# A four-layer graph network on one core: the last block of nodes on 32-row tiles, fewer packing stages in narrow chunks, narrower fetches

## The chip, the cores and the metric

The kernel runs on one core of a Trainium2 chip. The metric is the device time of one execution in microseconds (us), lower is better. Three executions of the kernel before took 2365.87, 2366.54 and 2370.38 us, so the median is 2366.54 us. A profile is one further execution, with its own time. In it, PE is TensorE's matmul, PEld its weight load, DVE is VectorE, ACT is ScalarE, POOL is GpSimd and SP is SyncE, which issues most of the transfers.

## What is computed

There are N = 2708 nodes with 512 features each, and an adjacency matrix adj of zeros and ones, in which a row has about sixteen ones. Four layers follow each other; each adds its result to its input and normalises each row. Cut to what matters:

```python
deg = max((adj != 0).sum(-1), 1)
x = layernorm(x + relu(((adj + I) @ x / deg + x) @ W0 + b0))        # layer 0
x = layernorm(x + (dis[:, None] * adj * dis[None, :]) @ x @ W1.T + b1)  # layer 1
for W in W_stack:                        # layer 2: two attention layers on x
    Wh, Ws = split(y @ W)
    a = softmax(Wh @ Ws.T) * adj
    y = leaky_relu(a @ Wh + y)
x = layernorm(x + y)
x = layernorm(x + adj @ x @ W3 + b3)                                # layer 3
```

Layer 0 scales both sides of adj by the square root of the degree, which is not written out here; dis is the inverse square root of adj's row sum.

## The kernel before

**Blocks and chunks.** The 2708 nodes are padded to 22 blocks of 128. The last block, number 21, holds only 20 real nodes; the other 108 rows of it are zeros. The columns of adj are cut into six chunks (CH, L28): four of 512 columns, one of 384 and one of 276. The blocks form six groups (GROUPS, L30): four groups of four blocks, then two of three, so block 21 is the last of the last group.

**Layers 0, 1 and 3.** For each chunk k and each group g, in this order, step() (L1001) is called. It first readies the next group (before_products, which calls load, L724, for the group after the next, and prepare, L757, for the next), then issues the products of this group (multiply, L821), then one part of the end of the chunk before (ends, L1036: multiplication by the weights, layernorm, storing). A run.phase counts these parts: it is 0 after the first group of a chunk, and so on.

**The products with adj.** The rows x of a block are split into a high and a low half in a reduced format (halve, L713: ACT makes xh, DVE makes xl), so that two fast matmuls give the accuracy of a slow one. For a chunk there are four accumulators acc in PSUM, one for each quarter d of the 512 features, each a bank of its own. For each block there are four times two matmuls with 128 rows of contraction, xh or xl as stationary operand and m, the block's piece of adj, as moving operand.

**Where m comes from.** Layer 0 loads adj transposed (at<-in_adj_t on SP), casts it to m on ACT, checks it on DVE (odd), adds up degrees (part) and writes it as bytes to a scratch in DRAM (masks; POOL casts and stores). Layers 1 and 3 and the attention read those bytes again (at<-mask, a<-mask). In layer 1, prepare also reduces the bytes on DVE to feeds: for each node, whether it feeds any node of each quarter (32 columns) of each block.

**The packing job.** index() (L1054) turns feeds of a chunk into lists of the nodes that feed a block of 128 nodes. Each block has eight lists of 128 places for nodes that feed one quarter only (two for each quarter) and four for the rest. The job is a generator in stages: a DVE stage, then a PE stage, in turn. First rank, then rest (both count places with matmuls), then for each block of the chunk one list: DVE builds a one-hot matrix (at_row, hit, both), PE sums it up (22 matmuls into list), and DVE copies the sum out of PSUM (sums), behind the one-hot of the list after it. The jobs of layer 1's chunks form a queue. work("PE") and work("DVE") advance the first job by one stage if it is that engine's turn. In layer 1, step() calls them at four places each in a chunk. What is left runs in the attention part, where beat() is called after each piece of work and advances a DVE stage and a PE stage every third time. A list must be there before the chunk is used in the attention.

**The attention.** Scores sp are computed by chunks, made into weights s by exp, multiplied by adj, and stored in DRAM next to the features: pairs holds for each pair of blocks and each node one row of 128 weights for the even block, 512 features, and 128 weights for the odd block. fetch() (L1524) gathers 128 such rows of one list by an indirect transfer on POOL into a tile g: the first or the last 640 elements of the row. weigh() (L1568) multiplies: for one of the rest lists one matmul with 128 columns of weights; for the four quarter lists of one turn, four matmuls, each with 32 columns of weights and an own 32 rows of PSUM (128*32 in the profile), next to each other.

**Order.** The Ordered wrapper (L53) fixes each engine's order to the order in which the program is written, so nothing is moved by a scheduler; line 70 stands for nearly every instruction in the profile, and groups are told apart by their tiles.

Of the kernel before, what the change touches and what calls it, by code (L numbers as in the profile page):

```python
# [513 lines left out]
class Fast:  # L514
# [198 lines left out]
    def halve(self, ly, j):  # L713

        nc = self.nc
        hi = self.page(f"xh{ly.number}_{j}", FR)
        lo = self.page(f"xl{ly.number}_{j}", FR)
        s = self.k.dis[:, j : j + 1] if ly.number == 1 else 1.0
        x = ly.rows[j]
        nc.scalar.activation(hi, x, AF.Copy, scale=s)  # L720
        nc.vector.scalar_tensor_tensor(lo, x, s, hi.bitcast(FP), ALU.mult, ALU.subtract)
        ly.hi[j], ly.lo[j], ly.rows[j] = hi, lo, None

    def load(self, ly, k, g):  # L724

        c0, cw = CH[k]
        if (k, g) in ly.loaded:
            return
        ly.loaded.add((k, g))
        js = range(*GROUPS[g])  # L730
        if ly.number == 0:
            tiles = []
            for j in js:
                at = self.wide(f"at{ly.number}_{k}_{j}")
                self.nc.sync.dma_start(at[:, :cw], self.k.adj_t[bass.ts(j, P), c0 : c0 + cw])
                tiles.append(at)
        else:
            at = self.page(f"at{ly.number}_{k}_{g}", U8, (P, DC, BANK))
            self.nc.sync.dma_start(
                at[:, : len(js), :cw], self.k.masks[k][:, js[0] : js[-1] + 1, :]  # L740
            )
            tiles = [at[:, q, :] for q in range(len(js))]
            ly.done["bytes", k, g] = at
        ly.done["at", k, g] = tiles
        if k == 0 and ly.number == 0:
            for j in range(*GROUPS[g]):
                self.load_rows(ly, j)
        if k == 0 and ly.number == 3 and g < 4:
            for j in range(*GROUPS[g]):
                self.load_rows(ly, j)  # L750
        if ly.number == 0 and g == 2:
            xt = [self.page(f"xt{k}_{c}") for c in range(DC)]
            for c in range(DC):
                self.nc.gpsimd.dma_start(xt[c][:, :cw], self.k.x_t[:, c, c0 : c0 + cw])
            ly.done["xt", k] = xt

    def prepare(self, ly, k, g):  # L757


        nc, (c0, cw) = self.nc, CH[k]  # L760
        ats = ly.done.pop(("at", k, g), None)
        if ats is None:
            return
        ms = []
        for j, at in zip(range(*GROUPS[g]), ats):
            if k == 0:
                self.halve(ly, j)
            m = self.page(f"m{ly.number}_{k}_{j}", FR)
            nc.scalar.copy(m[:, :cw], at[:, :cw])
            ms.append(m)  # L770
        ly.done["m", k, g] = ms
        if ly.number == 0:
            self.examine(ly, k, g, ats)
        if ly.number == 1:
            at, (j0, j1) = ly.done.pop(("bytes", k, g)), GROUPS[g]
            feeds = self.k.feeds.rearrange("p i q j -> p j (i q)")
            i0, full = c0 // QW, cw // QW
            for q0, q1, n in ((0, full, QW), (full, -(-cw // QW), cw % QW)):
                if q0 < q1:
                    v = at[:, : j1 - j0, q0 * QW : q0 * QW + (q1 - q0) * n]  # L780
                    nc.vector.tensor_reduce(
                        feeds[:, j0:j1, i0 + q0 : i0 + q1],
                        v.rearrange("p j (q i) -> p j q i", i=n),
                        AX.X,
                        ALU.max,
                    )

    def examine(self, ly, k, g, ats):
        nc, cw = self.nc, CH[k][1]
        b0 = GROUPS[g][0]  # L790
        if g == 0:
            ly.part[k] = self.page(f"part{k}", BF, (P, 2, BANK))
        odd = self.page(f"odd{k}_{g}", BF)
        at_b = self.page(f"bytes{k}_{g}", U8, (P, DC, BANK))
        for q in range(0, len(ats), 2):
            some = self.page(f"some{k}_{g}_{q}", BF, (P, 2, BANK))
            m = min(2, len(ats) - q)
            for h in range(m):
                at = ats[q + h][:, :cw]
                n = k * NB + b0 + q + h  # L800
                nc.scalar.copy(some[:, h, :cw], at)
                nc.vector.scalar_tensor_tensor(
                    odd[:, :cw],
                    at,
                    1.0,
                    at,
                    ALU.is_equal,
                    ALU.not_equal,
                    accum_out=self.k.bad[:, n : n + 1],
                )  # L810
            nc.gpsimd.tensor_copy(at_b[:, q : q + m, :cw], some[:, :m, :cw])
            p = ly.part[k][:, :m, :cw]
            if b0 + q == 0:
                nc.vector.tensor_copy(p, some[:, :m, :cw])
            else:
                nc.vector.tensor_add(p, p, some[:, :m, :cw])
        nc.gpsimd.dma_start(
            self.k.masks[k][:, b0 : b0 + len(ats), :], at_b[:, : len(ats), :cw]
        )

    def multiply(self, ly, k, g, only=None, ds=range(DC)):  # L821
        nc, cw = self.nc, CH[k][1]
        blocks = only or range(*GROUPS[g])
        two = ly.number == 3 and k < TWO
        starts, stops = ((0, 16), (15, NB - 1)) if two else ((0,), (NB - 1,))
        if blocks[0] in starts and 0 in ds:

            half = 0 if two and blocks[0] == 0 else k
            ly.acc[k] = [self.bank(half, f"acc{ly.number}_{k}_{d}") for d in range(DC)]
        ms = ly.done["m", k, g]  # L830
        todo = [(d, j) for d in ds for j in blocks]
        if k == 0 and g + 1 < len(GROUPS):
            todo.sort(key=lambda a: a[1])
        for d, j in todo:
            for x, first in ((ly.hi, True), (ly.lo, False)):
                nc.tensor.matmul(
                    ly.acc[k][d][:, :cw],
                    x[j][:, bass.ts(d, P)],
                    ms[j - GROUPS[g][0]][:, :cw],
                    start=(j in starts and first),  # L840
                    stop=(j in stops and not first),
                )
# [158 lines left out]
    def step(self, run, t):  # L1001
# [6 lines left out]
        if ly.number == 1 and k == len(CH) - 1 and g in (2, 3, 4):  # L1008
            self.attention.begin(g - 2)
        self.multiply(ly, k, g)  # L1010
        if run.before and run.phase in (1, 3, 4, 5):
            self.work("PE")
        if run.before:
            self.ends(run, run.phase)
            run.phase += 1
            if run.phase in (3, 4, 5):
                self.work("DVE")
        if g == (4 if ly.number == 3 and k < TWO else 3):
            self.residual(ly, k)
# [34 lines left out]
    def index(self, k):  # L1054
# [100 lines left out]
        nc.vector.tensor_single_scalar(part, whole, 7, op=ALU.arith_shift_right)  # L1155
        nc.vector.tensor_copy(which, part)
        sums = tile_("sums", [P, n, 2 * LISTS], FP)
        ps = None
        for q in range(n + 1):
            if q < n:  # L1160
                rows, both = self.one_hot(i0 + q, row[:, q, :], which[:, q, :])
            if ps is not None:
                nc.vector.tensor_copy(sums[:, q - 1, :], ps)
            if q == n:
                break
            yield "PE"
            ps = self.bank(self.other, f"list{i0 + q}", (P, 2 * LISTS))
            for j in range(NB):
                nc.tensor.matmul(
                    ps,  # L1170
                    rows[j // 8][:, j % 8, :],
                    both[:, j, :],
                    start=(j == 0),
                    stop=(j == NB - 1),
                )
            yield "DVE"
        t = tile_("list", [P, n, LISTS], FP)
        nc.vector.scalar_tensor_tensor(
# [58 lines left out]
class Attention:  # L1237
# [286 lines left out]
    def fetch(self, ch):  # L1524
# [5 lines left out]
        if q not in ch.x:  # L1530
# [3 lines left out]
            if ch.ly.number == 1:  # L1534
                ch.first[q] = self.page(f"x1{ch.name}_{q}")
                self.nc.sync.dma_start(ch.first[q][:w], self.k.saved[1][i][:w])
        self.nc.gpsimd.indirect_dma_start(
            out=g,
            out_offset=None,
            in_=ch.ly.pairs[ch.k % 2].rearrange("r j d -> (r j) d"),  # L1540
            in_offset=bass.IndirectOffsetOnAxis(ap=self.k.givers[:, i, t : t + 1], axis=0),
            element_offset=(q // 2) * NP * (D + 2 * P) + (q % 2) * P,
        )

        begin = max(self.fetch_free, self.clock + (16 if (q, t) == ch.first_fetch else 0))
# [22 lines left out]
    def weigh(self, wait=False):  # L1568
# [15 lines left out]
        gs = [ch.fetched.pop(0)[0] for _ in ts]  # L1584
        if first:
            ch.acc = self.bank(1, f"acc{ch.name}_{q}")
        c = (q % 2) * D
        for h, g in enumerate(gs):
            lo, m = (0, w) if len(gs) == 1 else (h * QW, QW)
            nc.tensor.matmul(  # L1590
                ch.acc[lo : lo + m],
                g[:, c + lo : c + lo + m],
                g[:, P - (q % 2) * P : P - (q % 2) * P + D],
                start=first,
                stop=last,
            )
# [206 lines left out]
```

## Time and profile before

| what | value |
|---|---|
| median of three executions | 2366.54 us |
| the profiled execution: its time, its span | 2390.8 us, 2388.9 us |
| mean granted TensorE clock | 0.989 |
| ACT busy, share of the span | 655.3 us, 27% |
| POOL busy, share of the span | 761.0 us, 32% |
| products acc<-m,xh and acc<-m,xl, instructions | 1584 and 1584 |
| moved by the transfers | 471.75 MB |

How to read it: the busy times of the engines overlap, so they don't add up to the span. Layer 0 runs from about 20 to 312 us after the span's start, layer 1 to 636, the attention to about 2170 (with the first products of layer 3 among its end), layer 3 to the end. A matmul of the full-precision kind (scores, weights) shows as two records of 429 ns each at 512 columns.

### The profile page before, as it was taken

The page shows a single profiled execution, that of the slowest core. Times are in us where ns is not written, and L with a number is a line of the kernel's source. Part 1 is how long each engine was busy: PE and PEld are TensorE (multiplying, and loading weights), DVE is VectorE, ACT ScalarE, POOL GpSimd, SP SyncE. Part 2 cuts the span into 40 slices and gives each one's busy share as a digit, 9 for nine tenths or more (in the row PEclk, how much of TensorE's full clock was granted, in tenths as well). Part 3 has the DMA queues.
Part 4 walks back from the last instruction along what each step waited for, and adds up shares of the span by engine and source line. Part 5 has one row for each costly group of instructions (what it writes and reads, how often), then busy time and mean ns, then how long its engine had stood idle before and what let it go on. Part 6 is the DMA issues. An engine that isn't in the chain of part 4 may idle for free.

```text
span 2388.9 us, 26130 instructions
## 1 busy us (share of the span) xinstructions
PE 2305.8 (97%) x8518; PEld 1315.5 (55%) x8518; DVE 1476.1 (62%) x2842; ACT 655.3 (27%) x1300; POOL 761.0 (32%) x879
## 2 busy tenths in 40 slices
PE   9999999999999999999999999999999989899997
PEld 6677777777644444443555344444343445566585
DVE  7989986787655328667667511238778777624513
ACT  6434352222100123222223200123232323431221
POOL 6545541111000001535456450001535556451000
PEclk9999999999999999999999999999999999999999
DMA  9754552222345405869789896405869799882311
GB/s 352 254 185 161 182 171 77 74 82 65 130 159 183 150 0 162 283 215 317 244 299 348 272 397 233 147 5 179 283 209 308 264 301 336 277 288 96 118 49 42
DMA packets 312151, 471.75 MB, mean 197 GB/s; under 512 B 59874, under 2 KB 189418, under 8 KB 312004
## 3 DMA queue, kind: packets, MB, share of 16 engines
q1 hardware_dynamic: 251988, 240.80, 30.7%
q0 software_dynamic: 60016, 229.18, 27.4%
q8 instruction: 69, 1.13, 0.2%
q14 instruction: 78, 0.64, 0.1%
HBM read 316.01 MB, written 153.85 MB: 197 GB/s over the span
## 4 chain that ended last, share of the span: by engine, by line
PE 83%; DVE 7%; issue 4%; DMA 3%; POOL 2%; ACT 1%; SPq 0%; another core or an unknown queue 0%; DVEq 0%; POOLq 0%; ACTq 0%
PE sp L70 30%; PE acc L70 30%; PE mm L70 9%; PE z L70 6%; PE wst L70 6%; POOL g L70 1%; DVE at_row L70 1%; DMA g<-pairs,givers 1%; DVE rs_t L70 1%; DMA at<-in_adj_t 1%; DVE feeds L70 0%; DVE st L70 0%; PE tr_x2b L70 0%; PE tr_x2t L70 0%; PE list L70 0%
## 5 line engine op out<-in xcount | busy, mean ns | idle before, releaser
L70 POOL DMA_INDIRECT g<-pairs,givers x510 | 516.3, 1012 | 922.1 <-issue 593.3
L70 PE MATMUL sp<-xs,wst_sb 128*128 128x512 f32 (+3 forms) x2112 | 798.2, 545 | 0.0
L70 PEld LDWEIGHTS sp<-xs,wst_sb 128*128 128x128 f32 (+1 forms) x2112 | 381.1, 186 | 408.6 <-issue 339.7
L70 PE MATMUL acc<-m,xh 128*128 128x512 f32 (+2 forms) x1584 | 586.8, 376 | 15.4 <-DVE dg L70 4.6
L70 PE MATMUL acc<-m,xl 128*128 128x512 f32 (+2 forms) x1584 | 571.1, 366 | 3.7 <-DVE xl L70 3.7
L70 PEld LDWEIGHTS acc<-m,xh 128*128 128x128 f32 x1584 | 299.3, 189 | 76.2 <-issue 16.1
L70 PEld LDWEIGHTS acc<-m,xl 128*128 128x128 f32 x1584 | 299.6, 189 | 52.5 <-issue 6.5
L70 PE MATMUL acc<-g 128*32 128x512 f32 (+1 forms) x1020 | 266.6, 605 | 6.8 <-issue 5.0
L70 DVE TENSOR_TENSOR top<-top,s 128x512 f32<-128x512 f32 (+5 forms) x240 | 149.4, 623 | 188.3 <-ACT s L70 129.9
L70 ACT COPY s<-sp 128x512 f32<-128x512 f32 (+2 forms) x252 | 133.4, 530 | 474.7 <-PE sp L70 312.6
L70 PE MATMUL mm<-w,ht 128*128 128x512 f32 (+1 forms) x528 | 227.3, 603 | 7.5 <-DVE ht L70 7.5
L70 ACT CAST m<-at 128x512 fp32r<-128x512 uint8 (+5 forms) x396 | 199.1, 566 | 79.2 <-DMA at<-mask 58.7
L70 ACT ACTIVATE s<-s 128x512 f32<-128x512 f32 (+3 forms) x264 | 150.5, 580 | 256.3 <-DVE s L70 169.6
L70 DVE TENSOR_TENSOR sum<-sum,s 128x512 f32<-128x512 f32 (+4 forms) x252 | 156.9, 622 | 38.7 <-ACT s L70 20.3
L70 DVE TENSOR_TENSOR s<-s,a 128x512 f32<-128x512 f32 (+3 forms) x264 | 165.8, 628 | 9.1
L70 PEld LDWEIGHTS mm<-w,ht 128*128 128x128 f32 (+1 forms) x528 | 97.3, 189 | 126.6 <-issue 113.1
L70 DVE TENSOR_TENSOR s<-s,shift 128x512 f32<-128x512 f32 (+3 forms) x264 | 162.7, 619 | 4.0 <-issue 4.0
L70 PE MATMUL wst<-xt,mixed 128*128 128x512 f32 (+2 forms) x384 | 157.2, 563 | 3.5 <-issue 3.5
L70 PEld LDWEIGHTS acc<-g 128*32 128x32 f32 (+1 forms) x1020 | 75.7, 134 | 148.2 <-issue 123.9
L70 PE MATMUL z<-w,xt 128*128 128x512 f32 (+1 forms) x352 | 150.8, 595 | 0.0
L70 POOL DMA_DIRECT2D x<-o x44 | 26.0, 596 | 370.2 <-DVE o L70 366.5
L70 DVE COPY z_sb<-z 128x512 f32<-128x512 f32 (+1 forms) x44 | 30.4, 690 | 179.3 <-PE z L70 140.9
(159 smaller groups left out, 1654.6 us busy)
## 6 DMA issues: line engine op xcount, KB each, us to landing
pairs<-s SPq DMA_DIRECT2D x378, 128.0 KB
pairs<-z_sb SPq DMA_DIRECT2D x84, 512.0 KB
at<-in_adj_t SPq DMA_DIRECT2D x88, 256.0 KB
xres<-x POOLq DMA_DIRECT2D x44, 256.0 KB
x<-o POOLq DMA_DIRECT2D x43, 256.0 KB
x<-x SPq DMA_DIRECT2D x37, 256.0 KB
at<-mask SPq DMA_DIRECT2D x32, 256.0 KB
xt<-t SPq DMA_DIRECT2D x32, 256.0 KB
```

The source lines that it names most:

```text
L70: ins = call(*args, **kw)
```

## The change

There are four parts.

1. **Block 21's products.** Its real nodes fit in 32 rows. In layer 0 its piece of adj is loaded four times, into rows 0 to 31, 32 to 63 and so on; the bytes stored for layers 1 and 3 then have the copies too. The new function fold() puts the four feature quarters of block 21 below each other, so that xh and xl of that block are 128 by 128. multiply() starts the last group with eight matmuls of 32 rows of contraction, two for each quarter d, each on its own 32 rows of the array and into its own accumulator; the others of the group follow. Degrees (part) and feeds count 32 rows of block 21 alone; for that the reduction of the last group is cut in two.
2. **Packing stages.** In chunks narrower than 512 columns, step() calls work("PE") at phases 1 and 5 instead of 1, 3, 4 and 5, and work("DVE") at phase 4 instead of 3, 4 and 5 (the one at the end of a chunk stays).
3. **Sums.** ACT copies a list's sum out of PSUM right after its matmuls; the copies on DVE are gone.
4. **Fetches.** A quarter list's fetch leaves out the weights of quarters that it doesn't use: from the list's own quarter on for an even block, up to and with it for an odd block. The tile's columns in weigh() follow.

```diff
@@ halve, fold @@
+        if j == NB - 1:
+            x, s = self.fold(ly, x, s)
+            hi, lo = hi[:, :P], lo[:, :P]
...
+    def fold(self, ly, x, s):
+        nc = self.nc
+        f = self.page(f"fold{ly.number}")[:, :P]
+        for d in range(DC):
+            nc.scalar.copy(f[d * QW : (d + 1) * QW], x[:QW, bass.ts(d, P)])
+        if ly.number == 1:
+            t = self.small.tile([P, 1], FP, tag="dis_f", name="dis_f")
+            for d in range(DC):
+                nc.vector.tensor_copy(t[d * QW : (d + 1) * QW], s[:QW])
+            s = t
+        return f, s
@@ load @@
-                self.nc.sync.dma_start(at[:, :cw], self.k.adj_t[bass.ts(j, P), c0 : c0 + cw])
+                if j < NB - 1:
+                    self.nc.sync.dma_start(
+                        at[:, :cw], self.k.adj_t[bass.ts(j, P), c0 : c0 + cw]
+                    )
+                    continue
+                few = self.k.adj_t[j * P : j * P + QW, c0 : c0 + cw]
+                for d in range(DC):
+                    self.nc.sync.dma_start(at[d * QW : (d + 1) * QW, :cw], few)
@@ prepare @@
+            sets = [(j0, j1, P)] if j1 < NB else [(j0, j1 - 1, P), (j1 - 1, j1, QW)]
...
-                if q0 < q1:
-                    v = at[:, : j1 - j0, q0 * QW : q0 * QW + (q1 - q0) * n]
+                for a, b, rows in sets if q0 < q1 else ():
+                    v = at[:rows, a - j0 : b - j0, q0 * QW : q0 * QW + (q1 - q0) * n]
                     nc.vector.tensor_reduce(
-                        feeds[:, j0:j1, i0 + q0 : i0 + q1],
+                        feeds[:rows, a:b, i0 + q0 : i0 + q1],
@@ examine @@
-            p = ly.part[k][:, :m, :cw]
+            n = QW if b0 + q == NB - 1 else P
+            p, t = ly.part[k][:n, :m, :cw], some[:n, :m, :cw]
@@ multiply @@
-        starts, stops = ((0, 16), (15, NB - 1)) if two else ((0,), (NB - 1,))
+        starts, stops = ((0, 16), (15, NB - 2)) if two else ((0,), (NB - 2,))
...
+        if blocks[-1] == NB - 1:
+            blocks = blocks[:-1]
+            for x in (ly.hi, ly.lo):
+                for d in range(DC):
+                    few = slice(d * QW, (d + 1) * QW)
+                    nc.tensor.matmul(
+                        ly.acc[k][d][:, :cw],
+                        x[NB - 1][few],
+                        ms[-1][few, :cw],
+                        start=False,
+                        stop=False,
+                    )
@@ step @@
-        if run.before and run.phase in (1, 3, 4, 5):
+        wide = CH[k][1] == BANK
+        if run.before and run.phase in ((1, 3, 4, 5) if wide else (1, 5)):
             self.work("PE")
...
-            if run.phase in (3, 4, 5):
+            if run.phase in ((3, 4, 5) if wide else (4,)):
                 self.work("DVE")
@@ index @@
-        ps = None
-        for q in range(n + 1):
-            if q < n:
-                rows, both = self.one_hot(i0 + q, row[:, q, :], which[:, q, :])
-            if ps is not None:
-                nc.vector.tensor_copy(sums[:, q - 1, :], ps)
-            if q == n:
-                break
+        for q in range(n):
+            rows, both = self.one_hot(i0 + q, row[:, q, :], which[:, q, :])
             yield "PE"
...
+            nc.scalar.copy(sums[:, q, :], ps)
             yield "DVE"
@@ fetch @@
+        h = t // ONLY if t < QUARTERS * ONLY else (0, QUARTERS - 1)[q % 2]
+        first, width = (P, D + (h + 1) * QW) if q % 2 else (h * QW, D + P - h * QW)
         self.nc.gpsimd.indirect_dma_start(
-            out=g,
+            out=g[:, :width],
...
-            element_offset=(q // 2) * NP * (D + 2 * P) + (q % 2) * P,
+            element_offset=(q // 2) * NP * (D + 2 * P) + first,
@@ weigh @@
-        c = (q % 2) * D
         for h, g in enumerate(gs):
             lo, m = (0, w) if len(gs) == 1 else (h * QW, QW)
+            e, z = (D + lo, 0) if q % 2 else (0, P - lo)
             nc.tensor.matmul(
                 ch.acc[lo : lo + m],
-                g[:, c + lo : c + lo + m],
-                g[:, P - (q % 2) * P : P - (q % 2) * P + D],
+                g[:, e : e + m],
+                g[:, z : z + D],
```

More of the change, by code (lines that the diff above doesn't have):

```diff
@@ L811, in examine @@
             nc.gpsimd.tensor_copy(at_b[:, q : q + m, :cw], some[:, :m, :cw])
-            p = ly.part[k][:, :m, :cw]
+            n = QW if b0 + q == NB - 1 else P
+            p, t = ly.part[k][:n, :m, :cw], some[:n, :m, :cw]
             if b0 + q == 0:
-                nc.vector.tensor_copy(p, some[:, :m, :cw])
+                nc.vector.tensor_copy(p, t)
             else:
-                nc.vector.tensor_add(p, p, some[:, :m, :cw])
+                nc.vector.tensor_add(p, p, t)
         nc.gpsimd.dma_start(
```

## The prediction

> **What bounds the kernel now.** I read the page's busy table and slices first, then TensorE's groups by shape, the windows by stage, TensorE's waits, and last the timeline where it waits.
>
> ```profile
> PE 2305.8 (97%) x8518; PEld 1315.5 (55%) x8518; DVE 1476.1 (62%) x2842; ACT 655.3 (27%) x1300; POOL 761.0 (32%) x879
> ...
> DVE  7989986787655328667667511238778777624513
> ```
>
> TensorE (PE) has work nearly always, so time is saved by taking PE work or PE waits away. But VectorE (DVE) stands at 8 to 9 tenths in the first slices, which is layer 0: there DVE may take over. Windows: stretch, length, then each engine's busy time.
>
> ```profile
> 62.00:316.00 254.00, 244.49 (x1066) 183.34 (x1066) 238.59 (x490) 107.72 (x234) 142.08 (x185) 0.99 0.61 199
> 316.00:637.00 321.00, 308.76 (x1585) 232.54 (x1584) 239.67 (x475) 88.72 (x185) 42.85 (x76) 0.99 0.30 97
> ...
> 2170.00:2366.00 196.00, 193.18 (x819) 142.67 (x820) 69.69 (x156) 42.00 (x96) 8.60 (x16) 0.98 0.23 72
> ```
>
> Layer 0 after its first chunk: PE 244 and DVE 239 of 254 us, two engines at once. Layer 1: PE 309 of 321, DVE 240. Layer 3: PE alone (193 of 196). The price of one product with adj is the distance between two starts, not the bar's length, since bars overlap:
>
> ```profile
> 457.00 0.39 PE L70 MATMUL acc<-m,xh 128*128 128x512 f32 x1
> 457.23 0.39 PE L70 MATMUL acc<-m,xl 128*128 128x512 f32 x1
> 457.46 0.39 PE L70 MATMUL acc<-m,xh 128*128 128x512 f32 x1
> ```
>
> 0.227 us each at 512 columns; the same reading gives 0.173 at 384 and 0.128 at 276. PE's waits in the two narrow chunks of layer 1 (us in total, times, longest):
>
> ```profile
> PE list L70 <- DVE both L70: 2.9, 2, 2.5
> PE acc L70 <- DVE sums L70: 2.7, 1, 2.7
> PE rest L70 <- DVE up L70: 1.9, 1, 1.9
> PE rank L70 <- DVE up L70: 1.2, 1, 1.2
> ```
>
> All 8.7 us come from the packing job of index(), whose DVE stage does not fit beside a narrow group. Why, on DVE's timeline:
>
> ```profile
> 582.70 3.22 DVE L70 TENSOR_TENSOR at_row<-upto,row 128x1024 bf16<-128x1024 bf16 x3
> 585.84 0.42 DVE L70 TENSOR_TENSOR hit<-upto,which 128x264 bf16<-128x264 bf16 x1
> 586.30 0.29 DVE L70 TENSOR_SCALAR both<-hit,node 128x264 bf16<-128x264 bf16 x1
> 586.51 0.43 DVE L70 TENSOR_TENSOR both<-hit,block 128x264 bf16<-128x264 bf16 x1
> ```
>
> One list's one-hot takes 4.2 us; a group of 24 products at 384 columns is over in 24 x 0.173 = 4.15 us.
>
> **What the Trainium skill says.** "TensorE: Matmul & The Clock Gate", Part 3 (measured speedup): four row tiles with K=32 and 512 columns ran 3.07 times as fast as in sequence, and weight loads run ahead of matmuls in flight only where the row group differs. This trace has no row tiles of this kind; its column tiles agree in kind: four 128*32 matmuls start 7 ns apart, the next four 453 ns after the first (1082.16 and 1082.61), where one full matmul of that type takes 429. The same page, LDWEIGHTS: loading 32x128 costs as much as 128x128 (columns count). Here a 128-column load lasts 189 ns, a 32-column one about 108; no 32x128 is shown. "TensorEngine Tiling (Array Packing)", Key Properties: a change of mode drains the array. The trace agrees: full to column tile starts 523 ns apart instead of 429, and back likewise; at 20-row transposes the extra is 93 ns too. "DMA: Bandwidth & Descriptors", Specifications: full rate needs at least 512 B; the narrowed rows keep 2176 B or more, so I expect no loss there.
>
> **1. Block 21 on row tiles.** Each of 18 chunks (six in layers 0, 1 and 3) swaps 8 full matmuls (4 column blocks d, hi and lo) for two sets of four 32-row tiles. Before: 8 x 0.227 = 1.82 us (wide), 1.38 (384), 1.02 (276). After: 0.093 in, two sets at one pitch plus 3 x 7 ns (0.248, 0.194, 0.149), 0.093 out: 0.68, 0.57, 0.48. Saved: 1.135, 0.81, 0.54. Bounds for a visit: 0.59 (1.82/3.07, no drain) below; above, 2.0 if the tiles run one by one with drains, and 3.5 if each also shows its 189 ns load. I take 0.68, since column tiles show the concurrency here.
> What remains per layer:
> - Layer 3: DVE has 70 us of 196. All counts: 4 x 1.135 + 0.81 + 0.54 = 5.9.
> - Layer 0, chunk 0: nothing. The last group waits for xl, m of blocks 19 to 21 (PE starts it at 55.18 and gets block 21's low half at 57.60). Block 21 now comes first, so PE starts at about 57.7 and ends where it ended (61.9). Four fold copies on ACT (0.2 to 0.4 us each by its small and 276-column copies) can add up to 0.5 us here; a 128-column xl gives about 0.4 back.
> - Layer 0, other chunks: DVE waited for PE's degree matmul 3.05, 1.07 and 2.03 us at the ends of chunks 1, 2, 3, so these keep 1.1 each. At chunk 4 DVE arrived 0.3 us late, and at chunk 5 PE waited 3.0 us for it: savings there are lost. Total 3.3.
> - Layer 1: chunk 0 full; chunk 1 keeps 0.25, as its second list's one-hot ended at 423.8 and PE came at 424.2; chunk 2 keeps 0.8 (DVE's up was done 0.8 before rest); chunk 3 full (DVE 5 us early); narrow ones full once part 2 empties DVE. 1.135 + 0.25 + 0.8 + 1.135 + 0.81 + 0.54 = 4.7.
> Sum 13.9 us. Costs hidden: fold's 4 ACT copies (and 4 tiny DVE ones in layer 1), a group ahead of use in layers 1 and 3; 3 more DMA issues per chunk of layer 0 on SP (18 x 0.35 us over 310 us, same bytes; uncovered they would delay a group's at tiles by 1 us); the split reduction of feeds, some 0.2 us of DVE per chunk.
>
> **2. Packing stages in narrow chunks.** Four PE stages become two there. The order of the built program shows it: rank, then rest at the chunk's end (384); two lists (276). Gone: the 8.7 us above, and PE's slow restart after two of them: in mm at 600.36 to 602.92 and wst at 637.3 to 639.9 seven pairs of starts lie 0.85 apart instead of 0.43, 2.9 us. Together 11.6. The PE work itself moves and costs the same. The queue then runs two stage pairs late per narrow chunk, and its last three lists come beside the first scores of attention. What is late next: the 3.9 us wait before a list at 690.2, behind DVE's layernorm, stays, with rest in its place (its DVE stage is 4.4 us against 4.2: -0.2). The wait of 1.4 at 794.9 becomes 1.1. The first list beside the scores is new: from z_20's end PE does z_21 (1.05) and one score block (8 x 0.429), 4.5 us; DVE does the z copy, index arithmetic and one-hot, 0.95 + 6.0. PE waits 2.5. The next two have 7.9 us for 4.3 of one-hot and up to 2.8 of adds. Net 11.6 - 0.2 + 0.3 - 2.5 = 9.2. Bounds: 3 (if other DVE work fills the same holes) and 11.6.
>
> **3. Sums on ScalarE.** 22 COPY sums of 0.18 us leave DVE, hidden there except where a bank waits for one queued behind the next one-hot: 2.7 us (in part 2) and 1.1 at 430.1. Gain 1.1. On ACT the copy waits for its list, in order; behind it stand ht copies and the m casts of the group after next, 4 x 0.52 = 2.1 us, wanted a whole group later (4.06 us at the narrowest). Nothing; uncovered, up to 0.8 us at each of 22.
>
> **4. Narrow fetches.**
>
> ```profile
> L70 POOL DMA_INDIRECT g<-pairs,givers x510 | 516.3, 1012 | 922.1 <-issue 593.3
> ```
>
> 336 of the 510 carry on average 192 B of 2560 less per row: 8.3 MB of 167. POOL still issues 510, 1 us each. PE's holes before acc<-g that a fetch may cause sum to some 9 us; 7.5% of a landing is a few tenths for few of them. I take 0.5, bounds -2 (rows start at 128 B steps, not seen here) and +2.
>
> **Sum.** 13.9 + 9.2 + 1.1 + 0.5 = 24.7 of the span of 2388.9: 2364.2. That execution took 2390.8, 24 us above the median of 2366.54; the same saving from the median gives 2341.8.
>
> **Rivals.** A: DVE takes PE's place in layers 0 and 1. Its 239 of 254 us speak for it, its waits for PE against. Only layer 3's 5.9 is left of part 1: 16.7 saved, 2349.8. B: packing finds the same holes elsewhere (part 2 gives 3 or less; for it, 11 stages in attention without slack shown): 18.5 saved or less, about 2350. C: row tiles run one by one, 2.0 a visit: part 1 loses 3.3 and 7.5 stay, 2359. D, slower: a row tile's 128-column load is not hidden behind its neighbours: 8 x (0.189 + 0.227) + 0.19 = 3.5 a wide visit, 1.7 more than before, and the same at 384 and 276: 18 x 1.7 = 30.6 lost against 10.8 gained, 2386. It decides from 1.82 + 10.8/18 = 2.4 us a visit. Against it: loads of column tiles start 7 ns apart. That the change does not do what it says is excluded for the order, not for the concurrency (C, D).
>
> **How the numbers follow.** Forecast 0.50, A 0.19, B 0.13, C 0.09, D 0.06; 0.03 for mishaps between. Own range of the forecast: part 1 from 10 to 17, part 2 from 6 to 11.6, fetches -2 to 2: 2335 to 2351. The range for 8 in 10 takes in A, B and most of C: 2332 to 2358. A change of 0.2% (4.7 us) is about what a measurement of this kernel can tell from none. Faster: forecast, A, B and nearly all of C, 0.90. Same: 0.03. Slower: D and a rest, 0.07.
>
> **What would show it.** Eight acc<-m starts of 32 rows spanning under 0.6 us between full ones, 0.09 drains at both ends (part 1; C and D show 1.8 to 3.3). No PE waits for both, up or sums from 560 to 640, and one of about 2.5 us beside the first scores. PE waits for dg after layer 0's chunks 4 and 5, longer by 0.5 to 0.8. PE's holes before acc<-g unchanged within 2 us. Wrong would be tiles not overlapping, or new waits of PE for DVE in layers 0 and 1 of more than 4 us.

## The result, and the profile after

The changed kernel took 2339.04 us (median of five runs, 2338.2 to 2344.43), the kernel before, run beside it, 2366.54 us (2356.57 to 2370.38). The medians lie 27.5 us apart; the ratio, in which all runs of both count, is 0.9896 with a 95% interval of 0.9871 to 0.9922: faster by 24.6 us, 18.5 to 30.5. The forecast was 24.7 us and 2342.

The page's busy table and the slices of DVE, after the change:

```profile
PE 2274.8 (97%) x8518; PEld 1292.5 (55%) x8518; DVE 1474.8 (63%) x2831; ACT 662.2 (28%) x1334; POOL 762.3 (33%) x879
...
DVE  6999986786655529657677511228677788724523
```

PE is still the bound, DVE's sum is the same, and ACT has the copies of fold and of the sums. The slices of layer 0 are as full of DVE as before: part 1 took PE work away beside an engine that is busy for nearly all of that stretch. Windows of layer 0 after its first chunk, of layer 1 and of layer 3 (stretch, length, then the busy time of PE, PEld, DVE, ACT and POOL):

```profile
62.00:312.00 250.00, 241.80 (x1075) 178.78 (x1073) 239.02 (x490) 109.58 (x237) 143.20 (x187) 1.00 0.63 203
312.00:616.00 304.00, 300.56 (x1536) 225.05 (x1537) 225.59 (x437) 89.50 (x196) 43.40 (x78) 0.99 0.32 104
2120.00:2312.00 192.00, 186.83 (x819) 135.19 (x820) 71.23 (x162) 43.30 (x101) 9.15 (x18) 0.99 0.24 77
```

In layer 1 PE is now idle for 3.4 of 304 us; before it was 12.2 of 321. (Two lists and a rank stage moved from there into the attention, so the shorter stretch is not all gain.) In layer 0 DVE has 239 of 250 us. Now the row tiles, on PE's timeline in layer 3:

```profile
2230.89 0.39 PE L70 MATMUL acc<-m,xh 128*128 128x512 f32 x1
2231.12 0.39 PE L70 MATMUL acc<-m,xl 128*128 128x512 f32 x1
2231.44 0.51 PE L70 MATMUL acc<-m,xh 32*128 32x512 f32 x4
2231.77 0.41 PE L70 MATMUL acc<-m,xl 32*128 32x512 f32 x4
2232.11 0.50 PE L70 MATMUL acc<-m,xh 128*128 128x512 f32 x1
2232.44 0.39 PE L70 MATMUL acc<-m,xl 128*128 128x512 f32 x1
2232.67 0.39 PE L70 MATMUL acc<-m,xh 128*128 128x512 f32 x1
```

Four tiles do run together (x4 on one line; they start 3 to 7 ns apart). But four distances are long, not two: 0.32, 0.33, 0.34, 0.33, where full matmuls take 0.227. From 2231.12 to 2232.44 it is 1.32 us; without block 21 those two steps take 0.45. So the visit costs 0.87 us, not 0.68, and saves 0.95, not 1.135. At 384 and 276 columns the same count gives 0.76 and 0.65, so 0.63 and 0.38 saved (forecast 0.81 and 0.54). The weight loads of the same stretch show where the second long distance behind each change comes from:

```profile
2231.43 0.19 PEld L70 LDWEIGHTS acc<-m,xh 32*128 32x128 f32 x4 [0.35 <-issue]
2231.54 0.19 PEld L70 LDWEIGHTS acc<-m,xl 32*128 32x128 f32 x4
2232.11 0.19 PEld L70 LDWEIGHTS acc<-m,xh 128*128 128x128 f32 x1 [0.37 <-issue]
2232.21 0.19 PEld L70 LDWEIGHTS acc<-m,xl 128*128 128x128 f32 x1
2232.45 0.19 PEld L70 LDWEIGHTS acc<-m,xh 128*128 128x128 f32 x1
```

In the stream the next weights start to load within 0.01 us of a matmul's start (2232.44 and 2232.45). Behind a change of mode the first matmul starts together with its own load, and the next load starts 0.11 us later (2231.54 and 2232.21); the matmul that needs it is late by as much.

PE's waits from 640 to 880 us, where the rest of the packing and the start of the attention lie (us in total, times, longest):

```profile
PE rest L70 <- DVE up L70: 4.1, 1, 4.1
PE list L70 <- DVE both L70: 3.0, 2, 2.7
PE rank L70 <- DVE up L70: 0.6, 1, 0.6
PE tr_mx L70 <- DVE wide L70: 0.3, 1, 0.3
```

From 560 to 640 the same view has no line at all: the 8.7 us of before are gone. The 4.1 us for rest is the wait that stood there before a list (3.8 us then), the 2.7 is the new one beside the first scores. POOL's gathers, last:

```profile
L70 POOL DMA_INDIRECT g<-pairs,givers x510 | 516.2, 1012 | 897.0 <-DMA pairs<-s 537.4
```

510 issues of 1012 ns, as before, though 8.3 MB less are fetched.

The two profiles differ by 52 us of span and not by 25. The profile before came from an execution of 2390.8 us, the profile after from one of 2338.2. The runs below came from three chips, on which the same kernel before took 2365.29, 2388.36 and 2392.58 us, so each is compared only with its own chip.

### The profile page after: what moved, and what is told of

Read it like the earlier page. It is cut to its first block, busy times and chain, and to the rows that moved or that the text cites. A ratio compares the mean times of both kernels' runs of the same rounds, so it can differ in the third digit from the quotient of the medians.

```text
span 2336.5 us, 26171 instructions
## 1 busy us (share of the span) xinstructions
PE 2274.8 (97%) x8518; PEld 1292.5 (55%) x8518; DVE 1474.8 (63%) x2831; ACT 662.2 (28%) x1334; POOL 762.3 (33%) x879
## 4 chain that ended last, share of the span: by engine, by line
PE 84%; DVE 7%; DMA 4%; issue 2%; ACT 1%; POOL 1%; SPq 0%; DVEq 0%; ACTq 0%; POOLq 0%
PE sp L70 32%; PE acc L70 29%; PE mm L70 9%; PE z L70 6%; PE wst L70 6%; DMA pairs<-s 1%; DMA at<-in_adj_t 1%; DVE st L70 1%; DMA at<-mask 1%; ACT m L70 1%; DVE s L70 1%; PE list L70 1%; PE mix L70 0%; POOL bytes L70 0%; PE tr_x2t L70 0%
## 5 line engine op out<-in xcount | busy, mean ns | idle before, releaser
L70 POOL DMA_INDIRECT g<-pairs,givers x510 | 516.2, 1012 | 897.0 <-DMA pairs<-s 537.4
L70 PE MATMUL acc<-m,xh 128*128 128x512 f32 (+4 forms) x1584 | 571.4, 382 | 13.6 <-ACT m L70 7.0
L70 PE MATMUL acc<-m,xl 128*128 128x512 f32 (+4 forms) x1584 | 553.2, 367 | 1.5 <-DVE xl L70 1.5
L70 PEld LDWEIGHTS acc<-m,xh 128*128 128x128 f32 (+1 forms) x1584 | 290.3, 189 | 81.4 <-issue 22.3
L70 PEld LDWEIGHTS acc<-m,xl 128*128 128x128 f32 (+1 forms) x1584 | 290.3, 189 | 48.1 <-issue 5.7
L70 PE MATMUL acc<-g 128*32 128x512 f32 (+1 forms) x1020 | 260.8, 605 | 0.9 <-DMA g<-pairs,givers 0.5
L70 PE MATMUL mm<-w,ht 128*128 128x512 f32 (+1 forms) x528 | 222.6, 593 | 8.1 <-DVE ht L70 8.1
L70 DVE TENSOR_TENSOR s<-s,a 128x512 f32<-128x512 f32 (+3 forms) x264 | 165.9, 628 | 10.2 <-DMA a<-mask 1.2
L70 PE MATMUL wst<-xt,mixed 128*128 128x512 f32 (+2 forms) x384 | 152.5, 550 | 1.7 <-ACT mixed L70 1.7
```

Of the source, the lines that this page charges most:

```text
L70: ins = call(*args, **kw)
```

## The experiments

### The four parts, each alone

Each kernel is the one before with one part of the change. Their core:

```diff
# part 1 alone (with fold, load, prepare and examine as in the change)
+        if blocks[-1] == NB - 1:
+            blocks = blocks[:-1]
+            for x in (ly.hi, ly.lo):
+                for d in range(DC):
# part 2 alone
-        if run.before and run.phase in (1, 3, 4, 5):
+        if run.before and run.phase in ((1, 3, 4, 5) if wide else (1, 5)):
# part 3 alone
-                nc.vector.tensor_copy(sums[:, q - 1, :], ps)
+            nc.scalar.copy(sums[:, q, :], ps)
# part 4 alone
-            out=g,
+            out=g[:, :width],
```

> Part 1 alone: block 21 on row tiles, nothing else of the change. The forecast's theory (a visit saves 1.14, 0.81 or 0.54 us, what DVE does not take back): layer 0 3.3, layer 3 5.9, layer 1 4.7 less up to 1.3 in the two narrow chunks, whose packing waits stay here: 12.6 to 13.9 us, so about 2353 to 2354. The trace of the changed kernel shows 0.76 us a wide visit instead of 0.68, so 0.08 us x 18 = 1.4 less is possible: 11.2 at the low end. Rival A (DVE takes PE's place in layers 0 and 1): 5.9 us, 2360.6. If the missing 2.8 us of the result (27.5 saved, 24.7 forecast) are of this part, it saves 15 or more.

> Part 2 alone: two packing stages instead of four in the narrow chunks. Forecast: 9.2 us (11.6 us of waits and slow restarts gone in layer 1, 2.5 back in a new wait of PE before the first list beside the first scores): 2357. Rival B (the same holes elsewhere): 3 or less, 2363.5. The wait of 2.7 us of acc for sums needs no part 3 to go, since a group then has one stage less beside it; if it stays, 6.5.

> Part 3 alone: the 22 copies of list sums on ScalarE. Forecast: 1.1 us by itself, and here also the 2.7 us wait of acc for sums in the narrow chunks, which part 2 would else take away: 3.8 at most, 2362.7; a slow restart of TensorE behind that wait would go too, about 1.3 more. Rival (the sums were hidden on DVE): within 1 us of before, 2366.

> Part 4 alone: narrower rows of the quarter lists. Forecast: 0.5 us, bounds -2 to +2, so 2366. Rival F: the 2.8 us of the result above the forecast, and part of the 20 us by which the attention stages of the two profiles differ, come from earlier landings: 3 us or more, 2363 or less, with PE's holes before acc<-g of quarter lists gone in the trace. If both traces with and without it show the same holes, the difference in attention was of the one profiled execution of before.

Measured, beside 2365.29 us for the kernel before:

| kernel | median, us | ratio (95%) | saved by the ratio, us |
|---|---|---|---|
| part 1 alone | 2356.64 | 0.9960 (0.9946 to 0.9974) | 9.4 |
| part 2 alone | 2358.83 | 0.9967 (0.9958 to 0.9977) | 7.8 |
| part 3 alone | 2361.47 | 0.9983 (0.9973 to 0.9992) | 4.0 |
| part 4 alone | 2363.64 | 0.9991 (0.9980 to 1.0001) | 2.1 |

Part 1 is below even the low end of 11.2 that its expectation gave, but its interval (6.2 to 12.8) touches it; Rival A's 5.9 is just outside. (The 0.76 us a visit in that expectation leaves out the late second start behind the tiles; with it the visit is 0.87.) Part 2 saved more than Rival B's 3. Part 3 saved about the 3.8 us that its two waits come to, and its rival, 1 us or less, falls (interval 1.9 to 6.4). Part 4 saved something between nothing and 4.7.

Did the packing of the narrow chunks take part 1's saving back, as its expectation allowed for? PE's waits from 560 to 640 us with part 1 alone:

```profile
PE list L70 <- DVE both L70: 2.5, 1, 2.5
PE acc L70 <- DVE sums L70: 2.5, 1, 2.5
PE rest L70 <- DVE up L70: 2.3, 1, 2.3
PE rank L70 <- DVE up L70: 1.2, 1, 1.2
```

The waits of before are all there. The one for rest is longer (2.3 us against 1.9), but together they are 8.5 us against 8.7, so they don't explain what is missing. Layer 1 gains about as much from part 1 alone as from part 1 beside the others (3.2 and 2.8 us in the table of stages below). With part 3 alone the same view shows:

```profile
PE list L70 <- DVE both L70: 2.5, 1, 2.5
PE rest L70 <- DVE up L70: 1.8, 1, 1.8
PE rank L70 <- DVE up L70: 1.2, 1, 1.2
```

The wait of acc for sums is gone. With part 2 alone the view is empty. So this wait goes with either part, as expected, and the other three go with part 2 alone.

### The kernel before again, and one part left out

The kernel before and the changed kernel, each unchanged, and the changed kernel with part 4 or part 1 undone:

```diff
# without part 4
-            out=g[:, :width],
+            out=g,
# without part 1
-        if blocks[-1] == NB - 1:
-            blocks = blocks[:-1]
```

> The kernel before, unchanged, for a second profile. In its first profile the stretch of attention from the first top block to the first product of layer 3 took 1132 us; in the profiles of the four single parts it took 1110, 1114, 1115 and 1110, with and without part 4. If those 18 to 22 us were of that one execution, they are not there now (1110 to 1115, span about 2360 to 2366). Rival: every part removes them, and they are back: 1130 or more, span 2385 or more.

> The changed kernel again, with more runs. 2339 to 2342, ratio 0.989 to 0.990. The single parts saved 9.4 + 7.8 + 4.0 + 2.1 = 23.3 us by their ratios; 2.7 us of wait is counted in parts 2 and 3 both, so without any help of one part for another 20.6 would be left (2344.7); part 1 in the narrow chunks of layer 1, where packing waits took its saving back, can add 1.0 (0.63 + 0.38) once part 2 is there.

> Parts 1 to 3 without part 4. Forecast: 0.5 us more than all four (bounds -2 to +2); by the run of part 4 alone 2.1 (-0.2 to 4.7). Rival F: 4 us or more above all four, with PE's holes before acc<-g grown by as much.

> Parts 2 to 4 without part 1. The difference to all four is what part 1 is worth where packing no longer takes it back. By the visit as traced (1.32 us for four starts where two took 0.45, so 0.87 a wide visit and 0.95 saved; 0.63 and 0.38 at 384 and 276 columns): layer 3 4.8, layer 1 3.9, layer 0 2.9: 11.6 us more than all four, 2351 to 2353. By the forecast's prices 13.9 us, 2354 to 2355. Rival A: layer 3 alone, 5 to 6, 2346.

These four ran on another chip, and there the kernel before took 2388.36 us.

| kernel | median, us | ratio (95%) |
|---|---|---|
| before | 2388.57 | 1.0000 (0.9990 to 1.0010) |
| all four parts | 2370.41 | 0.9917 (0.9899 to 0.9935) |
| without part 4 | 2372.81 | 0.9918 (0.9896 to 0.9940) |
| without part 1 | 2375.27 | 0.9937 (0.9916 to 0.9957) |

The long attention of the first profile came back, and it also came back with all four parts in. So the rival's number all but came true (1129 us from the first top block to layer 3, where it named 1130) but not its reason: the 20 to 30 us go with the chip. Parts 2 and 3 alone, whose attention is that of the kernel before, took 1253.0 and 1250.9 us for it on the chip of the table above, the kernel before 1272.0 here. (From which chips the first two profiles came is not known, and single executions of one kernel on one chip differ too: without part 4 they took 2360.06 to 2374.38 us.) The same changed kernel, windows of the attention, first in the profile above, then on this chip:

```profile
871.00:2116.00 1245.00, 1232.01 (x3982) 594.70 (x3980) 757.52 (x1348) 348.44 (x654) 521.25 (x519) 1.00 0.75 253
```

```profile
872.00:2150.00 1278.00, 1242.35 (x3980) 599.28 (x3979) 756.27 (x1348) 347.57 (x654) 519.67 (x519) 0.99 0.74 247
```

The same work of DVE, ACT and POOL fits in, but the stretch is 33 us longer; before and behind it the two profiles agree within 2 us. PE works 10 us longer there and stands idle 23 us longer. The 10 us are its clock: over this stretch the trace grants 0.999 of full speed in the first profile and 0.991 in the second. For the idle time I take it that transfers land later on such a chip. The packets of the gathers' queue took 178 ns on average there in the first profile and 181 in the second, which points that way but is little, and the trace doesn't show the landings, so this stays open.

Part 4 is worth nothing that shows (0.9917 against 0.9918). PE's waits for g on this chip are 1.3 us with it and 1.8 without, so there was little that earlier landings could save, and Rival F falls by this; the intervals of the times alone, some 5 us either way, would leave room for it. Part 1 is worth 4.8 us by these ratios. With such intervals that excludes neither Rival A's 5 to 6 nor twice as much, so the stages of the profiles are the better measure.

**By stages.** Times between the same instructions in each trace: from the start to the last degree matmul of layer 0; from there to the first block of scores reduced; from there to the last product with g; and from there to the last product with W of layer 3.

| kernel | layer 0 | layer 1, first scores | attention | rest of layer 3 |
|---|---|---|---|---|
| before, three profiles of its code up to the attention | 311.5, 312.8, 310.8 | 577.6, 578.3, 575.6 | 1274.5, 1272.0 | 209.7, 207.8, 208.5 |
| part 1 alone | 312.7 | 574.4 | 1245.9 | 203.6 |
| part 2 alone | 312.4 | 569.2 | 1253.0 | 209.6 |
| part 3 alone | 311.2 | 571.3 | 1250.9 | 209.4 |
| part 4 alone (also counted as before, outside the attention) | 310.8 | 575.6 | 1247.1 | 208.5 |
| without part 1 | 310.3 | 566.2 | 1271.7 | 208.2 |
| all four: profile above; this chip | 308.0; 308.9 | 563.4; 563.2 | 1244.5; 1278.2 | 203.5; 204.9 |
| without part 4 | 310.1 | 563.3 | 1278.6 | 203.6 |

The second column scatters by 2.7 us among the three profiles of before, and by 0.2 among the three with parts 1 to 3. Against 577.6 (the middle of the three), part 1 alone saves 3.2, part 2 8.4, part 3 6.3, parts 2 and 3 together 11.4, and all 14.2. In layer 3, part 1 saves 5.4 (middle of 207.8 to 209.7 against middle of the kernels with it), and 4.7 if the changed kernel again, late and best of the next section are counted, whose layer 3 is the same (204.3 to 205.1). In layer 0 single profiles scatter by up to 4.7 us; the middles (311.3 without, 309.5 with part 1) differ by 1.8.

Layer 0 can be read more finely. Much of its scatter is one stretch behind PE's wait for ht near 75 us, in which PE runs at half pace and loses 1.7 us; half of all the profiles have it. Beside it the steps repeat closely. From one degree matmul to the next, chunks 2 and 3 took 54.07 us in each profile without part 1 and 53.14 to 53.16 in each with it and its tiles together: 0.92 us saved a chunk, and chunk 1 gives the same where PE keeps its pace. From chunk 1's degree matmul to the end of PE's wait for dg at the start of layer 1 it takes 193.4 us without part 1 and 191.4 to 192.0 with it, so chunks 4 and 5 add next to nothing. Chunk 0 loses: its first product with W starts at 73.8 to 75.8 us without part 1 (middle 75.0), at 75.8 to 77.3 with it (middle 76.3).

In the attention the difference between kernels on one chip is within its scatter.

### Row tiles at the end of layer 0's first chunk; the packing a beat earlier; the sets apart

Three edits of the changed kernel, run beside it on a third chip, where the kernel before took 2392.58 us:

```diff
# late: layer 0, chunk 0: block 21's tiles behind blocks 19 and 20
+        late = k == 0 and ly.number == 0
+            if not late:
+                tiles(ly.hi, False)
+                tiles(ly.lo, False)
...
+        if tail and late:
+            tiles(ly.hi, False)
+            tiles(ly.lo, True)
# best: late, and in beat()
             self.work(("DVE", "", "PE")[self.beats % 3])
+            if self.beats % 3 == 2:
+                self.work("DVE")
# apart, in place of late: high tiles ahead of, low tiles behind blocks 19 and 20
+            tiles(ly.hi, False)
...
+        if tail and late:
+            tiles(ly.lo, True)
```

> The changed kernel once more, as the base of the two runs beside it. Two runs of it so far gave ratios 0.9896 (0.9871 to 0.9922) and 0.9917 (0.9899 to 0.9935) to the kernel before of the same chip, on chips where that took 2366 and 2388 us. Theory that the saving depends on the chip: near 0.990 if the kernel before takes 2366 here, near 0.992 if it takes 2388. Rival: no dependence, 0.991 in any case.

> The changed kernel with the row tiles of block 21 at the end of layer 0's first chunk instead of at the start of its last group, and that group block by block. The forecast gave this chunk no saving because block 21 comes first and PE waits for its low half (3.1 us before the first tile in the trace). If that is the reason, the wait goes and the chunk ends up to 3 us earlier; as DVE is late at chunks 4 and 5, 0 to 2 us of it are left at the end of layer 0, so 0 to 2 us below the changed kernel. Rival A (DVE sets layer 0): nothing is left by the end of chunk 1.

> The same, and in the attention part DVE's packing stage issued right after PE's stage, a beat earlier. In the traces of the changed kernel PE waits 4.3 us for rest, whose DVE stage stands behind a layernorm, and 2.8 us for the first list beside the scores, whose one-hot stands behind a copy of z; behind both waits PE can restart at half pace (about 1.7 us each). If DVE's order is the cause, both waits shrink below 1 us and 6 to 10 us go; if DVE had no time for it (the stages then delay the layernorm or the copies of z, which PE waits for instead), 2 us or less.

> The changed kernel with the two sets of tiles apart: the high halves at the start of the last group, the low halves at its end, so two visits of one set for one of two. In the trace of the changed kernel a wide visit costs 0.87 us: 0.09 and 0.11 for the two changes of mode, twice 0.227 for the sets, and twice 0.11 for the second start after each change. Theory: the second start after a change is late because its weights could not be loaded ahead over the change, whatever the tiles are. Then the step from high tiles to the next full matmul is about 0.33, the one after it 0.335, and the two visits cost 0.53 each, 1.06. Rival: the low halves' loads wait for the row group's own matmul; then the starts after the low tiles, which follow a full matmul, show no second late start.

| kernel | median, us | ratio (95%) |
|---|---|---|
| all four parts again | 2374.07 | 0.9920 (0.9907 to 0.9933) |
| late | 2369.73 | 0.9908 (0.9893 to 0.9922) |
| best | 2363.88 | 0.9864 (0.9842 to 0.9886) |
| apart, one run | 2376.12 | |

**All again.** The saving is 19.1 us here, near 0.992 as the first theory said for a chip of 2388 us; but 0.9896 and 0.9920 overlap in their intervals, so that the saving depends on the chip is not shown.

**Late.** With the tiles first (the changed kernel on this chip), PE waits for ACT's m:

```profile
59.36 0.50 PE L70 MATMUL acc<-m,xh 32*128 32x512 f32 x4 [2.43 <-ACT m L70]
```

With the tiles last:

```profile
61.57 0.50 PE L70 MATMUL acc<-m,xh 32*128 32x512 f32 x4
61.91 0.40 PE L70 MATMUL acc<-m,xl 32*128 32x512 f32 x4
64.13 0.38 PE L70 MATMUL deg<-both,ones_b 128*128 128x512 bf16 x1 [1.82 <-DVE both L70]
```

The wait at the tiles is gone, and the same time is lost two lines further down: the degree matmul starts at 64.13, with the tiles first it started at 64.08. In this chunk DVE's sum of degrees sets the end, whatever PE does. Rival A is right here, and the end of layer 0 comes no sooner (309.9 us against 308.2; the 1.7 us between them are the stretch at half pace behind ht, which of the two only late's profile has). The 0.9908 against 0.9920 is inside the intervals and has no place in layer 0.

**Best.** Both waits are gone: from 640 to 880 us only one of 0.3 us is left. The stage from layer 0's end to the first scores shrank from 563.3 to 553.3 us, so by 10.0, most of it 4.1 + 3.0 + 0.6 of waits and 1.8 that PE lost at half pace behind the wait for rest. DVE had the time; only the order of its queue kept it from using it. By the ratios the kernel is 13 us below the changed one, by the medians 10.2, and its interval lies below that of the changed kernel. (Two of its six runs, 2350.76 and 2352.55, lie over 11 us below the other four, so the stage is the better measure.)

**Apart.** High tiles behind the products with W, and low tiles behind full ones (a line of x5 holds a full matmul and the four tiles, in either order):

```profile
2214.70 0.94 PE L70 MATMUL acc<-m,xh 32*128 32x512 f32 x5
2215.48 0.40 PE L70 MATMUL acc<-m,xl 128*128 128x512 f32 x1
2215.71 0.40 PE L70 MATMUL acc<-m,xh 128*128 128x512 f32 x1
...
2218.68 0.83 PE L70 MATMUL acc<-m,xl 128*128 128x512 f32 x5
2219.44 0.50 PE L70 MATMUL acc<-m,xh 128*128 128x512 f32 x1
2219.78 0.39 PE L70 MATMUL acc<-m,xl 128*128 128x512 f32 x1
```

From high tiles to the second full matmul it takes 0.78 us: 0.44 and 0.34. The low set has the same (0.32 in, 0.44 out, 0.34 to the next). So the second start is late after low tiles too, and the rival falls. My expectation of 0.33 for the step out was a slip: leaving the mode (0.10) and the late second start of entering it (0.11) fall on the same step, 0.44. One set's visit then costs 0.32 + 0.44 + 0.34 - 2 x 0.227 = 0.64, two of them 1.28 against 0.87 for the sets together. Both follow from one price: 0.41 us for going in and out, and 0.227 for each set. Where the low set stands right before another break the second visit costs less: in layer 0, where the degree matmul follows it, chunks 2 and 3 took 53.44 us with the sets apart and 53.15 with them together.

## Why the prediction was right, by its steps

**The total** was right within the interval (24.7 against 24.6), and that closeness is in part luck. Two errors hide in it: part 1 was forecast too high, parts 2 and 3 too low. And on the two other chips the ratios give 19.8 and 19.1 us.

**Part 1, the visit: a term of the sum was missing.** The step read "0.093 in, two sets at one pitch plus 3 x 7 ns, 0.093 out: 0.68". Concurrency and the drain in (0.091) were right; C (2.0 a visit) and D (3.5) fall. What it left out is that the second start after each change of mode is 0.11 us late. The trace of before shows the same behind PE's waits, so it could have been read there:

```profile
67.97 0.50 PE L70 MATMUL acc<-m,xh 128*128 128x512 f32 x1 [1.69 <-DVE dg L70]
68.31 0.39 PE L70 MATMUL acc<-m,xl 128*128 128x512 f32 x1
68.54 0.40 PE L70 MATMUL acc<-m,xh 128*128 128x512 f32 x1
```

The first matmul behind a break is drawn 0.50 us long instead of 0.39, and the next starts 0.34 later instead of 0.227. I had taken the price of the change of mode from column tiles of the slower kind, where the four after the next started 453 ns later for 429 and so hid it. The row 4x (K=32, 512 columns) of "TensorE: Matmul & The Clock Gate", Part 3, gives 3.07; this kernel shows 1.82/0.87 = 2.1 for two sets and a way in and out, and the measurement decides. The loads fit what the prediction drew from that page in one point: one of 32x128 lasts 183 ns on average, one of 128x128 189. In the other they don't: full matmuls that use the same rows start 0.227 us apart with 189 ns loads, so loads run ahead there too, and it is a break that holds them up. Each visit costs 0.19, 0.19 and 0.17 us more than forecast at 512, 384 and 276 columns.

**Part 1 by layers.** Layer 3: 5.9 forecast, 4.7 to 5.4 by the stages, 4.8 by the corrected visits. Layer 1: 4.7 forecast, 2.8 to 3.2 measured, 3.9 by the corrected visits. That a wide visit is worth what the timeline says is seen where nothing else acts: from one rank stage to the next, with two visits between, it takes 87.15 us in place of 89.05. Some of what is missing may lie at about 415 us: behind the wait of 1.24 us for a list PE runs at half pace in six of the eight profiles with part 1 and in none of the six without.

Layer 0: 3.3 forecast, 1.8 between the middles. Chunks 1 to 3 keep 0.92 each where 1.1 was forecast, and the savings of chunks 4 and 5 are lost, as forecast: PE's waits at their ends grew by 0.5 and 0.7 us (from 1.4 and 2.9, though profiles without part 1 show up to 3.3 at the second). The step that failed is "chunk 0: nothing". This chunk's first product with W comes 1.3 us later with part 1. The four fold copies, for which the prediction allowed 0.5 us, are these (all four parts on the second chip):

```profile
58.19 1.22 ACT L70 COPY fold<-x 32x128 f32<-32x128 f32 x4
```

They stand ahead of the last casts of the chunk, for which DVE's sum of degrees waits; that they are the cause was not tested by itself. The first tile was at 59.2 us, not at 57.7, as ACT's m was the last to come and not xl, and behind PE's wait for it stands DVE's sum of degrees (late shows it). So part 1 is worth some 8 to 10 us, not 13.9; alone it gave 9.4 (6.2 to 12.8).

**Rival A** was given 16.7 us saved and is wrong as a whole: layers 0 and 1 kept some 5 us of the 8 forecast. It is right for the first chunk of layer 0 and for the last two, where the forecast said so too.

**Parts 2 and 3: 10.3 forecast, 11.4 measured together.** All waits of the narrow chunks went, the wait beside the first scores was 2.7 where 2.5 was forecast, and the one behind the layernorm grew from 3.8 to 4.1, as forecast. The two slow restarts that went were mis-sized: the prediction counted 2.9 us in mm and wst, but each costs 1.7, so 3.4, as the products ahead of mm ran at half pace too (from 599.67 us). Part 2 alone gave 8.4 where 9.2 was forecast; I had priced restarts at half pace behind the waits that go, but none behind the one that comes (in its trace, pairs of starts of scores lie 0.85 us apart from 802.8 to 805.4). Part 3 alone gave 6.3: the two waits that I named (1.1 and 2.7), a shorter wait before the next list, and slow restarts behind them. Rival B (3 or less) falls.

**Part 4: 0.5 forecast, within its bounds.** PE waited for g only 0.2 to 3.3 us in all the traces, so the width of a row is not what bounds it there.

**The base.** The forecast took the saving off the median although its profile was 24 us above it. That was right for a saving of which nearly all lies outside the attention: the excess of that profile lies inside it.

## What to carry to other kernels

Price an interruption of TensorE's stream from a wait in the same trace: the distance to the second start behind it is longer, and a short visit in another tile mode pays this twice, once going in and once coming out. So put sets of tiles together, and next to a place where the stream is broken anyway (behind a list, where the second start of full matmuls is late too, two sets cost 0.76 us instead of 0.87).

Where PE waits for an engine that has time to spare, look at what stands ahead in that engine's queue: one call moved by a beat gave 10 us here, as much as all the row tiles.

When a wait goes, look for the next one behind it before counting a gain, and when the profile's own time differs from the median, find the stretch that holds the difference.

## What the runs showed of the hardware

- The same kernel took 2365, 2388 and 2393 us on three chips. The difference lies in the stretch of gathers and stores (1246 to 1253 us against 1272 to 1284, over all the kernels profiled there); the layers that only multiply differ by no more than the scatter. In that stretch the packets of the gathers' queue took 178 to 181 ns on average on the first chip and 181 to 185 on the other two.
- The second start of acc's matmuls after a break of their stream (a change of tile mode, a wait, small bf16 matmuls between) comes 0.31 to 0.36 us after the first instead of 0.227 at 512 columns. Behind a change or a wait the load of its weights starts 0.11 us after the first matmul, in the stream within 0.01 us.
- After waits of 1.2 us and more TensorE can run at half pace (pairs of starts 0.85 us apart instead of 0.43 in the full-precision kind) for about 3.4 us, at a loss of 1.7, but not in each execution: behind the wait for rest at 663 us it did so in every profile that has this wait, behind that for ht near 75 in half of them. "TensorE: Matmul & The Clock Gate", Part 1, has it that the clock is throttled by default and that some 3.4 us of work release it; the trace agrees, with 3.4 us.
- 8.3 MB less in 336 gathers changed neither POOL's time for an issue (1012 ns) nor PE's time in the attention beyond the scatter.
